# Squares product without Strassen, and a wait of GpSimd on VectorE's two-operand operations

## The chip, the cores and the metric

The kernel runs on one core of a Trainium2 chip. The metric is device time in microseconds (us), the median of several executions of the same program. Five engines run side by side and meet at semaphores: TensorE (PE; PEld is its weight load), VectorE (DVE), ScalarE (ACT), GpSimd (POOL) and SyncE (SP), which mainly issues transfers. ACT and POOL issue transfers too; the transfers that add to what already stands at their destination are issued by POOL.

## The reference

```python
out_lin = x @ lin_w.T + lin_b                                   # x: 1024 x 512
xv = jnp.einsum('bf,efm->bem', x, weight)                       # weight: 64 x 512 x 512
zp = jnp.einsum('bf,efm->bem', jnp.square(x), jnp.square(weight))
interaction = 0.5 * jnp.sum(jnp.square(xv) - zp, axis=1)
return out_lin + interaction                                    # 1024 x 512
```

All inputs are float32. Since the sum over e can be taken before the second product, the squares need only one product: square(x) times the sum over e of square(weight), a 1024 x 512 by 512 x 512 product. The first einsum is 64 times as large and is the bulk of the work.

## The kernel before

**Three stages on TensorE.** First the linear part, x times lin_w. Then the main stage, the products of x with all weights. Last the squares product. All results are kept transposed where that helps, and everything is split in halves in both matrix directions (quadrants A11, A12, A21, A22 of x; r counts the two halves of x's rows, which are the batch, and c the two halves of the output columns).

**Strassen.** All three products are done by one level of Strassen's scheme in Winograd's form: seven products of quadrants or of sums of quadrants in place of eight. `OPERAND` names the left operand of each of the seven: A11, A12, A22 and the sums R5, R6, R7, R3.

**Main stage.** The weights are taken in 32 parts (h = 0 to 31). For each part the seven products come in the order 1, 6, 2, 3, 7, 5, 4, where product 5 is already that of the next part. Each product has two halves of 512 batch rows (a pair of PSUM banks each, from a ring of four pairs `bank`). To get float32 accuracy from the fast fp32r matmul, each operand is written as pieces H (high), L (low) and K (a mixed small term), and a product is three passes: H times H and L times L are the "front", K times K is the "back". Between the front and the back the bank is scaled and added to (`stt`, line 367). The back of a product is issued `LAG` = 4 slots after its front. The pieces of the x operands (X1H to X7K) are made once at the start and stay. The pieces pH, pL, pK of the weights are made for each product by `split` (line 630): H by ACT, L by ACT and then POOL or DVE, K by POOL. They live in rings of three buffers. `finish` (line 683) squares the finished banks on ACT (`sq`) and reduces over e on DVE (`acc`). `w_squares` (line 623) squares the raw weights on ACT (`wsq`) and reduces them on DVE into `w2_sum`. For product 7, DVE first subtracts p5 from the bank (`w<-bank,p`).

**The squares product (lines 793 to 916).** `load_square` loads the quadrants of x again into free weight buffers, ACT squares them, and sums of them are built by ACT and adding transfers (`add_square`, `minus`). `column_sums` builds the sums of quadrants of `w2_sum` on POOL. Then `one_level` (line 505) issues the seven products 1, 2, 5, 6, 4, 7, 3 as plain float32 matmuls, line 523. The output tiles `o_name[r, c]` start as the linear part (`p<-lind`) plus the summed squares of xv (`p<-accd`, adding transfers on POOL), DVE adds the products into them (`into`, `columns`), and ACT's queue stores them.

**The order of the work.** `Plan` (line 41) holds all operations with costs and dependencies. TensorE's order is fixed by `key`. `forward` (line 146) lays out the other engines in modelled time, always the ready operation with the earliest due time (`latest`); `order` (line 123) repeats that 60 times with slightly moved due times and keeps the layout with the earliest modelled end. The program then issues each engine's operations in that order, so that on the chip each engine runs its list in order.

VectorE and GpSimd can block one another when VectorE reads two tensors from SBUF. Operations of that kind carry `both=True`. The plan lets such a VectorE operation stay `held` while GpSimd is busy, and it writes an extra wait (`op.after`, issued at line 921) into the next GpSimd operation in two cases:

```python
elif tensor and held is not None and held.latest < o.latest + self.YIELD:
    ends(DVE, held, now + held.costs[DVE])
    o.after, held = held, None
    ...
elif tensor and held is None and free[DVE] > now and running[DVE].both:
    o.after = running[DVE]
    ends(e, o, free[DVE] + cost)
```

In all other cases nothing but the data orders a GpSimd operation against VectorE's.

Of the kernel before, what the change touches and what calls it, by code (L numbers as in the profile page):

```python
# [18 lines left out]
P = 128  # L19
# [7 lines left out]
LAG = 4  # L27
ORDER = (1, 6, 2, 3, 7, 5, 4)
SPLIT = {**dict.fromkeys(range(1, 8), POOL), 2: DVE, 3: DVE}
X_SPLIT = {5: DVE, 6: DVE, 3: DVE, 7: DVE, 1: DVE, 2: "DMA", 4: "DMA"}  # L30
FIRST = {**dict.fromkeys(range(1, 8), POOL), 5: DVE}
SCALE = {1: "DVE", 5: "ACT"}
# [8 lines left out]
class Plan:  # L41
# [104 lines left out]
    def forward(self, chain):  # L146
# [4 lines left out]
        running = dict.fromkeys(pending)  # L151
        times = [self.HOP]
        done, late, nxt, wire, held, mark = [], 0.0, 0, [12.0], None, None

        def release(o):
            for e in o.costs:
# [52 lines left out]
        while len(done) < len(ops):  # L209
            now = heapq.heappop(times)  # L210
            moved = True
            while moved:
                moved = False
                for e in pending:
                    if free[e] > now + 1e-6:
                        continue
                    o = pick(e, now)
                    if e == POOL and held is not None and (o is None or o.move):
                        ends(DVE, held, now + held.costs[DVE])
                        held = None  # L220
                    if o is None:
                        continue
                    moved = True
                    if e == PE:
                        nxt += 1
                        if running[PE] and running[PE].emit:
                            mark = running[PE]
                        late = max(late, now - o.latest)
                    cost = o.costs[e]
                    o.start, o.engine = now, e  # L230
                    if o.move and o.emit and mark and now < self.EARLY[0] and now > max(
                        ready(o, e) + 0.3, free[e] + 0.1
                    ):
                        o.after = mark
                    tensor = e == POOL and not o.move
                    if e == DVE and o.both and free[POOL] > now + 0.05 and not running[POOL].move:
                        held, free[e], o.end = o, float("inf"), float("inf")
                    elif tensor and held is not None and held.latest < o.latest + self.YIELD:
                        ends(DVE, held, now + held.costs[DVE])
                        o.after, held = held, None  # L240
                        ends(e, o, free[DVE] + 0.15 + cost)
                    elif tensor and held is None and free[DVE] > now and running[DVE].both:
                        o.after = running[DVE]
                        ends(e, o, free[DVE] + cost)
                    else:
                        ends(e, o, now + cost)
                    for f in o.costs:
                        pending[f].discard(o.n)
                    done.append((o, e))
                    for x in o.succ:  # L250
                        left[x] -= 1
                        if not left[x]:
                            release(ops[x])
# [4 lines left out]
def kernel(  # L258
# [531 lines left out]


    out_dst = out.rearrange("(c p) b -> p c b", p=P)
    sq_home = {}
    for n, q in (("A21", "T"), ("A22", "w11"), ("A11", "w22"), ("A12", "w12")):
        sq_home[n] = raw[q]()
    for n, q in (("R5", "w11"), ("R6", "w21"), ("R3", "w12")):
        sq_home[n] = raw[q]()
    sq_home["R7"] = sq_home["A21"]

    def load_square(n, again=None):  # L800
        r, q = quads[n]
        o = sq_home[n]
        dma(buf[o], x_src[:, ts(q, KH), ts(r, H)], (), (o,))
        if again:
            act(buf[sq_home[again]], buf[o], AF.Square, (o,), (sq_home[again],))
        act(buf[o], buf[o], AF.Square, (o,), (o,))

    def add_square(n, m):
        o, i = sq_home[n], sq_home[m]
        dma_add(buf[o], buf[i], (i,), (o,))  # L810

    def minus(n, m):
        o, i = sq_home[n], sq_home[m]
        act(buf[o], buf[i], AF.Copy, (i,), (o,), scale=-1.0)

    load_square("A21")
    minus("A21", "A21")
    load_square("A22", "R5")
    add_square("R5", "A21")
    load_square("A11", "R6")  # L820
    add_square("R6", "R5")
    add_square("R7", "A11")
    load_square("A12")
    minus("R3", "A12")
    add_square("R3", "R6")
    w2 = {(r, c): w2_sum[:, ts(r, KH), ts(c, HM)] for r in range(2) for c in range(2)}
    w2_names = {z: (("w2h", *z),) for z in w2}
    for (r, c), ap in w2.items():
        plan.add({ACT: 0.6}, lambda _, ap=ap: nc.scalar.mul(ap, ap, -0.5),
                 tuple(("w2", r, m) for m in range(M)  # L830
                       if ("w2", r, m) in plan.writer and m // HM == c), w2_names[r, c])
    wt_home = [raw[q]() for q in ("w22", "T")]
    wt = {
        k: buf[wt_home[(k - 1) // 2]][:, (k - 1) % 2].rearrange("p (k m) -> p k m", k=KH)
        for k in range(1, 5)
    }
    wt_names = {k: (("wt", k),) for k in range(1, 5)}
    for z, n in enumerate(wt_home):
        used(n, ("wt", 2 * z + 1), ("wt", 2 * z + 2))
    column_sums(w2, wt, w2_names, wt_names,  # L840
                lambda o, a, b, r, w: pool(o, a, b, False, r, w, 512))
    act(wt[2], wt[2], AF.Copy, wt_names[2], wt_names[2], 512, -1.0)
    left = {i: (buf[sq_home[n]], (sq_home[n],)) for i, n in OPERAND.items()}
    right = rhs_of(w2, w2_names, wt, wt_names)

    turn(NG - 1)
    o_name = {}

    def acc_names(ch):
        return tuple(("accd", g, q) for g in range(NG) for q in range(P // MG)  # L850
                     if g * MG // P == ch)

    for (r, c), n in (((0, 0), "p1"), ((1, 0), "p1"), ((1, 1), "p5"), ((0, 1), "p5")):
        n = o_name[r, c] = kept[n]()
        for u in range(2):
            used((n, u), n)
        dma(buf[n], lin_dram[:, ts(c, 2), ts(r, H)], (("lind", r, c),), both_of(n))
        for u in range(2):
            ch = 2 * c + u
            if ch < M // P - 1:  # L860
                dma_add(buf[n, u], acc_dram[:, ch, ts(r, H)], acc_names(ch), ((n, u),), 1.4, 5.0)

    def into(n, bank, sub, u):
        o = buf[n][:, u]
        dve(o, o, buf[bank[u]], sub, ((n, u), bank[u]), ((n, u),))
# [5 lines left out]
    def columns(n, m, sub, u):  # L871
        o, i = buf[n][:, u], buf[m][:, u]
        dve(o, o, i, sub, ((n, u), (m, u)), ((n, u),), 512, True)

    v, f2, f5, f4 = four()
    f3 = f4[0], f2[0]
    key = slot[0]
    one_level(1, right, left, v, True, key)
    one_level(2, right, left, f2, True, key + 4)
    for u in range(2):  # L880
        into(o_name[0, 0], v, False, u)
        into(o_name[0, 0], f2, False, u)
        store(0, 0, u)
    one_level(5, right, left, f5, True, key + 6)
    z = kept["w"]()
    for u in range(2):
        used((z, u), z)
        act(buf[z, u], buf[f5[u]], AF.Copy, (f5[u],), ((z, u),), 512)
        for r in range(2):
            columns(o_name[r, 1], z, True, u)  # L890
    one_level(6, right, left, v, False, key + 8)
    for u in range(2):
        into(o_name[0, 1], v, True, u)
    one_level(4, right, left, f5, True, key + 11)
    for u in range(2):
        into(o_name[1, 0], f5, False, u)
    last = wsquare()
    for r in range(2):
        used((last, r), last)
    for r in (1, 0):  # L900
        dma(buf[last][:, r], acc_dram[:, M // P - 1, ts(r, H)], acc_names(M // P - 1),
            ((last, r),), 1.0)
        n = o_name[r, 1]
        stt(buf[n, 1], buf[last][:, r], 0.5, buf[n, 1], ALU.add, ((last, r), (n, 1)), ((n, 1),),
            512, True)

    one_level(7, right, left, v, False, key + 14)
    for u in range(2):
        into(o_name[1, 1], v, True, u)
        store(1, 1, u)  # L910
        into(o_name[1, 0], v, False, u)
        store(1, 0, u)
    one_level(3, right, left, f3, True, key + 17)
    for u in range(2):
        into(o_name[0, 1], f3, True, u)
        store(0, 1, u)

    for op, engine in plan.order():
        if op.emit:
# [40 lines left out]
```

## Time and profile before

| | |
|---|---|
| median of 3 runs | 1284.9 us (1284.19 to 1286.25) |
| the profiled execution, its own time | 1282.88 us |
| its span, first to last instruction | 1280.6 us |
| TensorE busy | 1275.7 us (100% of the span) |
| VectorE busy | 1230.9 us (96%) |
| ScalarE busy | 962.1 us (75%) |
| GpSimd busy | 1044.7 us (82%) |
| granted TensorE clock | 1.000 |

Matmuls are pipelined, so the busy time of one overlaps that of the next; what a matmul costs in a stream is the distance from one start to the next. A float32 matmul shows as two matmul records in the profile, an fp32r one as one record. Times after a line name (L702, L523) are from line numbers of the kernel before. "bank", "pL", "X6H" and the like are tile names with the buffer number left out; tiles that share storage show under the name of the storage, so that the squared quadrants appear as T and w, and the output tiles as p.

### The profile page before, as it was taken

The numbers are of one execution on the slowest core, as the hardware profiler recorded it, in microseconds if no ns is written. First come the engines' busy times: TensorE is split into PE (matmuls) and PEld (weight loads), VectorE is DVE, ScalarE is ACT, GpSimd is POOL, SyncE is SP. The second block draws the span as 40 slices with busy tenths as digits, with TensorE's granted clock in tenths as the row PEclk, the third lists the DMA queues.
The fourth block names the chain that finished last, engine by engine and source line by source line (L and its number), as shares of the span: only waits on it lengthen the run. The fifth ranks groups of instructions, "written<-read, shape, count | busy, mean of one in ns | idle before, by whom it ended". The sixth has DMA issues, their size and how long they took to land.

```text
span 1280.6 us, 15506 instructions
## 1 busy us (share of the span) xinstructions
PE 1275.7 (100%) x5484; PEld 1025.9 (80%) x5484; DVE 1230.9 (96%) x1021; ACT 962.1 (75%) x1006; POOL 1044.7 (82%) x531
## 2 busy tenths in 40 slices
PE   9999999999999999999999999999999999999998
PEld 4788888888888888888888888888888888888884
DVE  6999999999999999999999999999999999999996
ACT  7777787777887777877777877777788777778781
POOL 2988898888898888898888888888889888889891
PEclk9999999999999999999999999999999999999999
DMA  7765654455664555655445664545665445665656
GB/s 231 182 172 138 148 136 112 100 118 136 148 148 103 103 122 125 153 136 132 98 111 124 148 153 105 117 111 116 152 148 131 108 102 121 141 152 118 147 120 154
DMA packets 67645, 170.36 MB, mean 133 GB/s; under 512 B 22896, under 2 KB 23920, under 8 KB 67568
## 3 DMA queue, kind: packets, MB, share of 16 engines
q0 software_dynamic: 20160, 71.84, 30.5%
q1 hardware_dynamic: 45152, 94.39, 25.7%
q10 hardware_dynamic: 2256, 3.15, 0.7%
q8 instruction: 43, 0.70, 0.2%
q14 instruction: 34, 0.28, 0.1%
HBM read 158.86 MB, written 6.29 MB: 129 GB/s over the span
## 4 chain that ended last, share of the span: by engine, by line
PE 98%; DVE 1%; issue 0%; ACT 0%; ACTq 0%
PE bank L702 94%; PE bank L523 3%; PE bank L512 1%; DVE bank L367 0%; DVE acc L386 0%; PE bank L540 0%; DVE w_sum L386 0%; DVE w L373 0%; ACT sq L361 0%; DVE p L373 0%; ACTq L361 0%
## 5 line engine op out<-in xcount | busy, mean ns | idle before, releaser
L379 POOL TENSOR_TENSOR pK<-pH,pL 128x1024 fp32r<-128x1024 f32 x223 | 586.6, 2631 | 177.5 <-PE bank L702 169.4
L361 ACT ACTIVATE sq<-bank 128x1024 f32<-128x1024 f32 x256 | 261.6, 1022 | 95.4 <-issue 48.4
L386 DVE TENSOR_REDUCE acc<-sq 128x16 f32<-128x1024 f32 x256 | 308.0, 1203 | 0.7 <-ACT sq L361 0.7
L379 POOL TENSOR_TENSOR pL<-T,pL 128x1024 fp32r<-128x1024 f32 x95 | 237.9, 2504 | 1.0 <-ACT pL L361 1.0
L367 DVE SCALAR_TENSOR_TENSOR bank<-bank,w 128x1024 f32<-128x1024 f32 x192 | 234.1, 1219 | 0.4 <-PE bank L702 0.2
L373 DVE TENSOR_TENSOR w<-bank,p 128x1024 f32<-128x1024 f32 x128 | 155.6, 1216 | 26.0 <-PE bank L702 26.0
L379 POOL TENSOR_TENSOR pL<-w,pL 128x1024 fp32r<-128x1024 f32 x65 | 175.1, 2694 | 0.0
L361 ACT ACTIVATE p<-bank 128x1024 f32<-128x1024 f32 x128 | 131.0, 1023 | 56.3 <-PE bank L702 56.3
L367 DVE SCALAR_TENSOR_TENSOR pL<-pH,w 128x1024 fp32r<-128x1024 f32 x62 | 168.1, 2711 | 0.0
L361 ACT ACTIVATE pL<-T 128x1024 fp32r<-128x1024 f32 x95 | 100.0, 1053 | 74.5 <-issue 72.0
L386 DVE TENSOR_REDUCE w_sum<-wsq 128x16 f32<-128x1024 f32 x128 | 154.2, 1205 | 0.0
L367 DVE SCALAR_TENSOR_TENSOR bank<-bank,p 128x1024 f32<-128x1024 f32 x128 | 152.9, 1216 | 0.0
L361 ACT ACTIVATE pH<-w 128x1024 fp32r<-128x1024 f32 x127 | 134.2, 1057 | 11.6 <-PE bank L702 11.3
L361 ACT ACTIVATE wsq<-w 128x1024 f32<-128x1024 f32 x128 | 135.0, 1055 | 4.0 <-DVE w_sum L386 4.0
L361 ACT ACTIVATE pH<-T 128x1024 fp32r<-128x1024 f32 x96 | 101.3, 1055 | 0.0
L361 ACT ACTIVATE pL<-w 128x1024 fp32r<-128x1024 f32 x65 | 69.0, 1062 | 43.0 <-PE bank L702 25.0
L398 POOL DMA_DIRECT2D T<-weight x94 | 83.2, 978 | 9.2 <-POOL pL L379 9.0
L702 PE MATMUL bank<-pH,X4H 128*128 128x512 f32 x256 | 81.1, 397 | 0.1
L702 PE MATMUL bank<-pL,X4L 128*128 128x512 f32 x256 | 79.5, 391 | 0.0
L702 PE MATMUL bank<-pH,X5H 128*128 128x512 f32 x256 | 79.2, 391 | 0.0
L702 PE MATMUL bank<-pL,X5L 128*128 128x512 f32 x256 | 78.8, 389 | 0.0
L702 PE MATMUL bank<-pL,X6L 128*128 128x512 f32 x256 | 78.8, 389 | 0.0
(117 smaller groups left out, 2561.0 us busy)
## 6 DMA issues: line engine op xcount, KB each, us to landing
w<-weight SPq DMA_DIRECT2D x128, 512.0 KB, 7.7
T<-weight POOLq DMA_DIRECT2D x94, 512.0 KB, 7.4
w<-weight POOLq DMA_DIRECT2D x32, 512.0 KB, 10.3
T<-weight SPq DMA_DIRECT2D x31, 512.0 KB, 6.4
accd<-turned SPq DMA_DIRECT2D x64, 32.0 KB, 8.6
p<-lind SPq DMA_DIRECT2D x4, 512.0 KB, 6.2
out<-p ACTq DMA_DIRECT2D x8, 256.0 KB, 2.3
w<-xT SPq DMA_DIRECT2D x6, 256.0 KB, 4.9
```

What stands on the lines that cost most here:

```text
L361: nc.scalar.activation(o, i, func, bias=bias, scale=scale)
L367: return nc.vector.scalar_tensor_tensor(o, i, scalar, j, ALU.mult, op)
L373: return (nc.vector.tensor_sub if sub else nc.vector.tensor_add)(o, a, b)
L379: return (nc.gpsimd.tensor_sub if sub else nc.gpsimd.tensor_add)(o, a, b)
L386: lambda _: nc.vector.tensor_reduce(o, i.rearrange("p a (m e) -> p a m e", e=E), axis=AX.X, op=ALU.add),
L398: {POOL: 0.62}, lambda _: nc.gpsimd.dma_start(o, i, accum_op=ALU.add),
L512: return nc.tensor.matmul(buf[bank[u]], b[:, k, ts(u, P)], a[:, k, :], start=first and k == 0, stop=k == KH - 1, skip_group_check=True,)
L523: made = nc.tensor.matmul(buf[bank[u]], b[:, k, ts(u, P)], a[:, k, :], start=first and k == 0, stop=k == KH - 1, skip_group_check=True,)
L702: made = nc.tensor.matmul(buf[bank, j], buf[x][:, k, ts(2 * half + j, P)], buf[w][:, k, :], start=first and k == 0, stop=k == KH - 1, skip ...
```

## The change

Two things change.

The first is in `forward`. A variable `between` remembers the last two-operand VectorE operation that the plan has begun since the last GpSimd operation. When a GpSimd operation is laid out and has no extra wait yet, it gets one on that VectorE operation, even when the plan has it finished by then. The modelled times are not touched by this.

The second is the squares product. It is no longer Strassen's. The four output blocks (r, c) are computed one after the other, each as two products of quadrants (z = 0, 1), so eight block products, and each in three passes of fp32r matmuls on pieces H, L and K, as in the main stage. Passes 0 and 1 (H, L) of both z go to one pair of banks (`front`), pass 2 (K) to another (`back`); DVE scales each and adds it to the output tile. The pieces of the squares of x and of `w2_sum` are written over the x pieces X6, X2, X3 and X5, X1 of the main stage, which are not needed any more by then, and for A22 into one buffer of each ring of weight pieces. `SUMS` and `SQUARES` say who makes the L pieces: for `w2_sum` half 0 an adding transfer (the K piece too), for half 1 VectorE; for A11 and A12 GpSimd, for A21 and A22 an adding transfer. The K pieces of the squares are all made by GpSimd.

```diff
+SUMS = {0: "DMA", 1: DVE}
+SQUARES = {"A11": POOL, "A12": POOL, "A21": "DMA", "A22": "DMA"}
...
+        between = None
...
                     elif tensor and held is None and free[DVE] > now and running[DVE].both:
-                        o.after = running[DVE]
                         ends(e, o, free[DVE] + cost)
                     else:
                         ends(e, o, now + cost)
+                    if tensor:
+                        if o.after is None and between is not held:
+                            o.after = between
+                        between = held
+                    elif e == DVE and o.both:
+                        between = o
...
-    load_square("A21")
-    minus("A21", "A21")
...
-    column_sums(w2, wt, w2_names, wt_names,
-                lambda o, a, b, r, w: pool(o, a, b, False, r, w, 512))
...
+    for r, pieces in enumerate((("X5H", "X5L", "X5K"), ("X1H", "X1L", "X1K"))):
+        w2 = w2_sum[:, ts(r, KH)]
+        names = tuple(("w2", r, m) for m in range(M) if ("w2", r, m) in plan.writer)
+        sums[r] = h, l, k = pieces
+        act(buf[h], w2, AF.Copy, names, (h,), scale=-0.5 * TRIM)
+        if SUMS[r] == DVE:
+            stt(buf[l], w2, -0.5, f32(h), ALU.subtract, (h, *names), (l,), 1024, True)
+            stt(buf[k], f32(h), -U, f32(l), ALU.add, (h, l), (k,), 1024, True)
+        else:
+            half = (("w2h", r),)
+            act(w2, w2, AF.Copy, names, names + half, scale=-0.5)
+            act(buf[l], w2, AF.Copy, half, (l,), scale=-TRIM)
+            dma_add(f32(l), w2, half, (l,))
+            act(buf[k], w2, AF.Copy, half, (k,), scale=-U * TRIM)
+            dma_add(f32(k), f32(l), (l,), (k,))
+    for n, q, pieces in (
+        ("A11", "T", ("X6H", "X6L", "X6K")), ("A12", "w11", ("X2H", "X2L", "X2K")),
+        ("A21", "w22", ("X3H", "X3L", "X3K")), ("A22", "w12", [piece[z]() for z in "HLK"]),
+    ):
+        (r, z), o = quads[n], raw[q]()
+        dma(buf[o], x_src[:, ts(z, KH), ts(r, H)], (), (o,))
         act(buf[o], buf[o], AF.Square, (o,), (o,))
+        squares[r, z] = h, l, k = pieces
+        act(buf[h], buf[o], AF.Copy, (o,), (h,), scale=U * TRIM)
+        if SQUARES[n] == POOL:
+            act(buf[l], buf[o], AF.Copy, (o,), (l,), scale=TRIM)
+            pool(buf[l], buf[o], f32(l), True, (o, l), (l,))
+        else:
+            act(buf[l], buf[o], AF.Copy, (o,), (l,), scale=-TRIM)
+            dma_add(f32(l), buf[o], (o,), (l,))
+        pool(buf[k], f32(h), f32(l), True, (h, l), (k,))
...
-    for (r, c), n in (((0, 0), "p1"), ((1, 0), "p1"), ((1, 1), "p5"), ((0, 1), "p5")):
+    BLOCKS = (0, 0), (1, 0), (0, 1), (1, 1)
+    for (r, c), n in zip(BLOCKS, ("p1", "p1", "p5", "p5")):
...
+    def into(n, bank, scale):
+        stt(buf[n], buf[bank[0][0]], scale, buf[n], ALU.add, (*bank, *both_of(n)), both_of(n), 1024)
+
+    def into_half(n, bank, scale, u):
+        o = buf[n, u]
+        stt(o, buf[bank[u]], scale, o, ALU.add, (bank[u], (n, u)), ((n, u),))
...
-    one_level(1, right, left, v, True, key)
-    one_level(2, right, left, f2, True, key + 4)
...
+    def passes(which, r, c, bank, key):
+        for u in range(2):
+            for z in range(2):
+                def emit(_, u=u, z=z):
+                    for i in which:
+                        for k in range(KH):
+                            w, x = buf[sums[z][i]], buf[squares[r, z][i]]
+                            made = nc.tensor.matmul(
+                                buf[bank[u]], w[:, k, (2 * c + u) * P:(2 * c + u + 1) * P],
+                                x[:, k, :], start=z == 0 and i == which[0] and k == 0,
+                                stop=z == 1 and i == which[-1] and k == KH - 1,
+                                skip_group_check=True,
+                            )
+                    return made
+                reads = [t[i] for i in which for t in (sums[z], squares[r, z])]
+                plan.add({PE: len(which) * KH * PASS}, emit, (*reads, bank[u]), (bank[u],),
+                         key=key + 0.2 * u + 0.1 * z)
...
+    for at, (r, c) in enumerate(BLOCKS):
+        n = o_name[r, c]
+        front, back = b[2 * at % 4], b[(2 * at + 1) % 4]
+        passes((0, 1), r, c, front, key + 6 * at)
+        if at < 3:
+            into(n, front, S + 1.0)
+        if c == 1:
+            dma(buf[last][:, r], acc_dram[:, M // P - 1, ts(r, H)], acc_names(M // P - 1),
+                ((last, r),), 1.0)
+            stt(buf[n, 1], buf[last][:, r], 0.5, buf[n, 1], ALU.add, ((last, r), (n, 1)),
+                ((n, 1),), 512, True)
+        if at < 3:
+            passes((2,), r, c, back, key + 6 * at + 4)
+            into(n, back, S)
+        else:
+            into(n, front, S + 1.0)
+            back = back[0], b[0][1]
+            passes((2,), r, c, back, key + 6 * at + 4)
+            for u in range(2):
+                into_half(n, back, S, u)
+        for u in range(2):
+            store(r, c, u)
```

KH is 2 and P is 128: a pass of one u and one z is two matmuls of 128x128 weights and 512 columns.

More of the change, by code (lines that the diff above doesn't have):

```diff
@@ L792 @@
     out_dst = out.rearrange("(c p) b -> p c b", p=P)
[L793 to L805, printed above, removed]
-        act(buf[o], buf[o], AF.Square, (o,), (o,))
@@ L808, in add_square @@
[L808 to L814, printed above, removed]
-    load_square("A21")
-    minus("A21", "A21")
[L818 to L836, printed above, removed]
@@ L837 @@
-    wt_names = {k: (("wt", k),) for k in range(1, 5)}
-    for z, n in enumerate(wt_home):
-        used(n, ("wt", 2 * z + 1), ("wt", 2 * z + 2))
-    column_sums(w2, wt, w2_names, wt_names,
-                lambda o, a, b, r, w: pool(o, a, b, False, r, w, 512))
-    act(wt[2], wt[2], AF.Copy, wt_names[2], wt_names[2], 512, -1.0)
-    left = {i: (buf[sq_home[n]], (sq_home[n],)) for i, n in OPERAND.items()}
-    right = rhs_of(w2, w2_names, wt, wt_names)
+    squares, sums = {}, {}
+    for r, pieces in enumerate((("X5H", "X5L", "X5K"), ("X1H", "X1L", "X1K"))):
[13 more added lines that the diff above has]
+            dma_add(f32(k), f32(l), (l,), (k,))
@@ L846 @@
     turn(NG - 1)
-    o_name = {}
     def acc_names(ch):
@@ L851, in acc_names @@
                      if g * MG // P == ch)
-    for (r, c), n in (((0, 0), "p1"), ((1, 0), "p1"), ((1, 1), "p5"), ((0, 1), "p5")):
+    o_name = {}
+    BLOCKS = (0, 0), (1, 0), (0, 1), (1, 1)
+    for (r, c), n in zip(BLOCKS, ("p1", "p1", "p5", "p5")):
         n = o_name[r, c] = kept[n]()
@@ L861 @@
                 dma_add(buf[n, u], acc_dram[:, ch, ts(r, H)], acc_names(ch), ((n, u),), 1.4, 5.0)
-    def into(n, bank, sub, u):
-        o = buf[n][:, u]
-        dve(o, o, buf[bank[u]], sub, ((n, u), bank[u]), ((n, u),))
+    def into(n, bank, scale):
[3 more added lines that the diff above has]
+        stt(o, buf[bank[u]], scale, o, ALU.add, (bank[u], (n, u)), ((n, u),))
     def store(r, c, u):
@@ L869, in store @@
         dma(out_dst[:, 2 * c + u, ts(r, H)], buf[n, u], ((n, u),), (), 1.0, (SP, ACT))
[L871 to L877, printed above, removed]
-    one_level(1, right, left, v, True, key)
-    one_level(2, right, left, f2, True, key + 4)
[L880 to L896, printed above, removed]
+    def passes(which, r, c, bank, key):
[15 more added lines that the diff above has]
+                         key=key + 0.2 * u + 0.1 * z)
     last = wsquare()
@@ L899 @@
         used((last, r), last)
[L900 to L916, printed above, removed]
+    b = four()
+    key = slot[0]
+    for at, (r, c) in enumerate(BLOCKS):
[20 more added lines that the diff above has]
+            store(r, c, u)
     for op, engine in plan.order():
```

## The prediction

> **What bounds the kernel now.** I read the page's busy times first, then the chain of work that ended last, in order of time.
>
> ```profile
> PE 1275.7 (100%) x5484; PEld 1025.9 (80%) x5484; DVE 1230.9 (96%) x1021; ACT 962.1 (75%) x1006; POOL 1044.7 (82%) x531
> ```
>
> ```profile
> core 0 of [0], span 1280.6 us
> by line: PE bank L702 94.2%; PE bank L523 3.2%; PE bank L512 0.6%; DVE bank L367 0.4%; DVE acc L386 0.4%; PE bank L540 0.3%; DVE w_sum L386 0.2%; DVE w L373 0.2%; issue 0.1%; ACT sq L361 0.1%; DVE p L373 0.1%; ACTq L361 0.0%
> ...
> 66.84 1183.86 PE bank L702 x5208
> 1250.69 3.43 PE bank L523 x8
> 1254.13 1.86 PE bank L702 x8
> 1255.98 20.62 PE bank L523 x48
> 1276.60 0.02 issue
> 1276.62 0.69 DVE p L373
> ```
>
> TensorE at 100% proves little, since busy times of matmuls overlap. The chain proves it: from 66.84 us to 1276.60 it never leaves TensorE. VectorE is at 96% and GpSimd at 82%, yet neither ends a wait that the chain goes through. So only two things can move the time: fewer microseconds of matmuls, or new or removed waits of TensorE. How much waiting is left? The same chain asked for a late window alone gives the undisturbed step:
>
> ```profile
> 1224.86 25.84 PE bank L702 x114
> ```
>
> 25.84 / 114 = 0.2267 us from one fp32r matmul to the next. At that step the 5208 matmuls would take 1180.5 us; they took 1183.86. So 3.4 us, spread over the main stage, is all that better order could return there.
>
> **The matmuls.** The squares product now is line 523 after 1250 us: 3.43 + 20.62 = 24.05 us for 56 records, 28 float32 matmuls, 0.859 us each. The 1.86 us between are the last backs of the main stage and stay. New are 4 blocks x 2 u x 2 z x 3 passes x 2 = 96 fp32r matmuls, of the same form and size as those of line 702: 96 x 0.2267 = 21.76 us. The chain becomes shorter by 24.05 - 21.76 = 2.29 us. This is the main term. It is small because Strassen's saving (seven for eight) is given up while a float32 matmul costs 0.859 / 0.2267 = 3.8 passes and is replaced by three.
>
> The Trainium skill, "TensorE: Matmul & The Clock Gate", section "Wait — 56ns, not 53.3ns?", has warm back-to-back matmuls at N / 2.4 GHz plus about 2.5 ns, 0.2157 us for 512 columns; by that price the new product would be an estimated 20.7 us and the gain 3.3 us, over the bound for faster. The 5208 matmuls of this trace average 0.2273 us at the full granted clock, the new ones have the same form, and so I give that result no chance of its own.
>
> **The end.** After TensorE comes one VectorE addition, then a store.
>
> ```profile
> 1276.62 0.69 DVE L373 TENSOR_TENSOR p<-p,bank 128x512 f32<-128x512 f32 x1 [0.35 <-PE bank L523]
> ```
>
> ```profile
> L367 DVE SCALAR_TENSOR_TENSOR bank<-bank,p 128x1024 f32<-128x1024 f32 x128 | 152.9, 1216 | 0.0
> ```
>
> ```profile
> out<-p ACTq DMA_DIRECT2D x8, 256.0 KB, 2.3
> ```
>
> Let T be the end of TensorE. Now VectorE ends at T + 0.35 + 0.69 = T + 1.04. In the new last block the back is 8 matmuls, 1.81 us, so the front is done at T - 1.81 and its `into`, 1.22 us (price of the bank row), runs from T - 1.46 to T - 0.24. The two halves `into_half`, 0.69 each, follow: the first to T + 0.45, the second to T + 1.14. That is 0.10 us later. The stores keep number, size and landing time of 2.3 us; the last is one of eight as before. So +0.1.
>
> **What the new pieces cost the other engines.** Busy times of the last stretches:
>
> ```profile
> 1230.00:1240.00 10.00, 10.00 (x46) 8.28 (x45) 10.00 (x11) 8.99 (x11) 10.00 (x7) 1.00 0.63 132
> 1240.00:1250.50 10.50, 10.50 (x48) 8.60 (x47) 9.31 (x9) 4.60 (x5) 10.50 (x11) 1.00 0.83 164
> 1250.50:1276.60 26.10, 26.08 (x65) 11.98 (x64) 19.22 (x27) 4.05 (x5) 2.17 (x3) 1.00 0.59 145
> ```
>
> ```profile
> L361 ACT ACTIVATE w<-w 128x1024 f32<-128x1024 f32 x6 | 6.3, 1062 | 0.0
> ```
>
> The columns are PE, PEld, DVE, ACT, POOL. ScalarE: 12 operations for the four squares and 5 for `w2_sum`, 17 x 1.06 = 18.0 us, in place of eight squares and negations of the same price (8.5 us) and smaller ones: at most +9.5 us. It is idle for 1.0 + 5.9 us of the first two stretches and 22 us of the third, and only the pieces of A11, A12 and `w2_sum` are due by 1251. Cost on the path: nothing, under that cover; without it up to 9.5 - 6.9 = 2.6 us.
>
> ```profile
> L379 POOL TENSOR_TENSOR pK<-pH,pL 128x1024 fp32r<-128x1024 f32 x223 | 586.6, 2631 | 177.5 <-PE bank L702 169.4
> ```
>
> ```profile
> 1248.07 3.72 POOL L379 TENSOR_TENSOR T<-w_sum 128x512 f32<-128x512 f32 x1
> 1259.77 0.88 POOL L398 DMA_DIRECT2D p<-accd  x1 [7.97 <-DMA p<-lind]
> ```
>
> GpSimd: six subtractions of 2.63 us, 15.8 us, come in, and the four column sums (one is shown) go. The adding transfers are four before and four after, and the loads of x four and four. Due times, with the first new front at 1250.5: front 16 x 0.2267 = 3.63, old backs 1.81, so A11's K is due at 1255.9, A12's at 1256.4, A21's and A22's at 1261.4 and 1261.9; only the L of A11 and A12 are due by 1251. After 1250.5 the engine has 24 idle us now. Cost nothing, if the order in its queue is right (see the rivals).
>
> ```profile
> 1237.51 1.19 DVE L386 TENSOR_REDUCE w_sum<-wsq 128x16 f32<-128x1024 f32 x1
> ...
> 1246.35 1.22 DVE L386 TENSOR_REDUCE acc<-sq 128x16 f32<-128x1024 f32 x1 [0.36 <-ACT sq L361]
> 1248.01 1.22 DVE L373 TENSOR_TENSOR w<-bank,p 128x1024 f32<-128x1024 f32 x1 [0.44 <-PE bank L702]
> ```
>
> ```profile
> 1250.53 3.59 PE L523 MATMUL bank<-w,w_sum 128*128 128x512 f32 x8
> ```
>
> ```profile
> 1249.33 1.03 ACT L361 ACTIVATE sq<-bank 128x1024 f32<-128x1024 f32 x1 [1.68 <-DVE w L373]
> ```
>
> VectorE is the tight one. The last sum over `wsq` ends at 1238.70; then ScalarE makes H and VectorE makes L of half 1, due when z = 1 begins, 1250.5 + 0.9 = 1251.4. In that time VectorE also frees the first bank: `w<-bank,p` at 1248.01, ScalarE's square to 1250.36, and the tail's first matmul at 1250.53: under 0.2 us of play. L takes 1.2 us free and, behind a GpSimd operation, up to 3.4 us (next part). Its cover is the idle 0.36 and 0.44 and the reduction of 1.22, which nothing awaits at once: 2.0 us. So TensorE loses between 0 and 1.4 us here. I take 0.2, near the lower end, because the reduction alone covers an undisturbed L.
>
> **The new wait.** What is queued behind a waiting GpSimd operation is its whole list, and pK is what TensorE's backs need.
>
> ```profile
> L367 DVE SCALAR_TENSOR_TENSOR pL<-pH,w 128x1024 fp32r<-128x1024 f32 x62 | 168.1, 2711 | 0.0
> ```
>
> ```profile
> 416.89 3.02 POOL L379 TENSOR_TENSOR pK<-pH,pL 128x1024 fp32r<-128x1024 f32 x1
> 421.72 2.39 POOL L379 TENSOR_TENSOR pK<-pH,pL 128x1024 fp32r<-128x1024 f32 x1 [1.81 <-PE bank L702]
> ```
>
> ```profile
> 417.59 3.40 DVE L367 SCALAR_TENSOR_TENSOR pL<-pH,w 128x1024 fp32r<-128x1024 f32 x1
> ```
>
> ```profile
> 1225.29 1.78 DVE L367 SCALAR_TENSOR_TENSOR pL<-pH,w 128x1024 fp32r<-128x1024 f32 x1
> ```
>
> ```profile
> 1227.22 1.48 POOL L379 TENSOR_TENSOR w<-w_sum 128x512 f32<-128x512 f32 x1
> ```
>
> In the main stage the two-operand operations are these 62, two per part. At 417.59 VectorE begins while GpSimd works, and ends at 420.99, 1.08 us after GpSimd's 419.91: it was shut out. The next GpSimd subtraction starts at 421.72, 0.7 us after VectorE's end, because it awaited TensorE (a free buffer). The tightest of the 62 is the one at 1225.29: end 1227.07, GpSimd at 1227.22. In none does GpSimd begin inside one. The new wait is met before it is asked, 62 times. Cost zero; the collisions that exist are of the other kind (VectorE second), which this wait doesn't touch. If it did bind, GpSimd's 169 us of waiting for TensorE would cover it. Only at the start is there something to change:
>
> ```profile
> 36.20 3.22 POOL L379 TENSOR_TENSOR pK<-pH,pL 128x1024 fp32r<-128x1024 f32 x1 [1.25 <-DVE X6K L367]
> ```
>
> ```profile
> 35.95 1.21 DVE L373 TENSOR_TENSOR X7L<-w,X7H 128x1024 fp32r<-128x1024 f32 x1
> 37.09 3.42 DVE L373 TENSOR_TENSOR X3L<-w,X3H 128x1024 fp32r<-128x1024 f32 x1
> ```
>
> GpSimd began inside X7L, and X3L then lost 3.42 - 1.22 = 2.2 us to it. With the wait, VectorE could be up to 2.2 us earlier and GpSimd about 1 us later. Neither is on the chain there; I take zero, between a return of part of the 3.4 us (rival B) and +1.0.
>
> **Sum.** -2.29 + 0.10 + 0.2 + 0 = -2.0 us. Against the profiled execution: span 1280.6 to 1278.6, its time 1282.88 to 1280.9. The median of the runs is 2.0 above that execution, so 1284.9 becomes 1282.9, 0.16% less. About 0.2%, 2.57 us, is what a measurement of this kernel can tell from no change.
>
> **The rivals.** B, faster: the planner's list is laid out anew and the start is freed, and part of the 3.4 us lost in the main stage comes back too. At 0.6 of it the change passes 2.57; at 1.3 it gives 1281.6; all of it 1279.5. For it: VectorE's lost 2.2 us. Against: the loss recurs through the main stage, where the wait alters nothing. C, smaller gain: VectorE's L is shut out behind a GpSimd operation just before 1250, the full 1.4 us and, with K, as much again: 1284.1 to 1285.5. For it: that little play. D, slower: GpSimd's queue is in order, and its last `p<-accd` waited 7.97 us for a load, to 1259.77. If this one stands ahead of the K of A12, that K is ready only at 1259.8 + 0.9 + 2.6 = 1263.3, against 1256.4: TensorE waits 6.9 us, the sum is +4.7, 1289.6; with A11's K behind it as well 1292. If only A21's and A22's are behind, the loss is 4.0 us and the whole within the bound. It decides from 4.8 us of waiting. Against: the K pieces are due earlier than that addition, whose block now comes last, and the planner goes by due times; for: those are modelled times, and when a load lands is not in GpSimd's hands. E, the wait does nothing: that is in my sum already.
>
> **How the numbers follow.** Forecast 0.50 (1282.4 to 1283.5 by itself), B 0.23, C 0.14, D 0.13. Forecast and C lie within 0.2%: 0.64. The range 1281.2 to 1287.0 leaves out D (0.13) and the far end of B (0.06).
>
> **What would show it.** Right: the tail is 96 matmuls of 0.227 us without gaps, its first at about 1250.5; no waits of GpSimd for VectorE's pL in the table of waits; VectorE's last operation about 1.1 us behind the last matmul. Wrong: a gap of TensorE ahead of the first front or at a back, with GpSimd's pieces as releaser (D) or VectorE's L (C); a main stage under 1182 us (B); or a matmul step that differs in the tail.

## The result and the profile after

| | before | after |
|---|---|---|
| median (20 runs each) | 1284.45 us | 1281.99 us |
| lowest and highest run | 1282.77, 1286.25 us | 1281.12, 1283.26 us |
| the profiled execution, its own time | 1282.88 us | 1282.14 us |

The ratio is 0.9981, with a 95% interval of 0.9975 to 0.9987: 2.5 us less, between 1.7 and 3.2. That is about at the bound of what this kernel's measurement can tell from no change. Forecast were 1282.9 us, 2.0 us less.

The busy times of the kernel after, in the columns of the page:

```profile
PE 1274.3 (100%) x5524; PEld 1033.4 (81%) x5524; DVE 1233.0 (96%) x1014; ACT 967.0 (76%) x1008; POOL 1053.9 (82%) x533
```

No engine has changed its place. The count of TensorE is right for the change: 5484 - 56 + 96 = 5524. The chain of work that ended last, in order of time (start, duration, what), has changed at its end. Lines after the edit: 710 is the old 702, 870 issues the new passes, 375 is the old 367; in the experiments the numbers shift by a few lines.

```profile
67.63 1164.97 PE bank L710 x5126
...
1246.24 1.12 DVE acc L394
1247.36 2.62 DVE X1K L375
1249.98 1.15 DVE w L381
...
1251.21 1.03 ACT sq L369
...
1252.29 3.92 PE bank L870 x16
1256.21 1.81 PE bank L710 x8
1258.02 16.34 PE bank L870 x72
1274.38 1.24 DVE p L375
...
1275.71 0.69 DVE p L375
```

Before, the chain stood on TensorE up to the last addition. Now it leaves TensorE in front of the squares product, for VectorE: `X1K` (the K piece of the second half of `w2_sum`), then `w<-bank,p`, then ScalarE's square, which frees the bank that the first new front wants. The timeline of TensorE shows the hole that this makes (idle time before, and its releaser, in brackets):

```profile
1250.24 1.07 PE L710 MATMUL bank<-pK,X7K 128*128 128x512 f32 x4
1252.29 0.73 PE L870 MATMUL bank<-X6H,X5H 128*128 128x512 f32 x2 [0.97 <-ACT sq L369]
```

And the timelines of GpSimd and VectorE show why `X1K`, 1.2 us of work, took 2.71 us:

```profile
1245.53 3.36 POOL L387 TENSOR_TENSOR pK<-pH,pL 128x1024 fp32r<-128x1024 f32 x1
...
1250.07 2.97 POOL L387 TENSOR_TENSOR X6K<-X6H,X6L 128x1024 fp32r<-128x1024 f32 x1
```

```profile
1247.27 2.71 DVE L375 SCALAR_TENSOR_TENSOR X1K<-X1H,X1L 128x1024 fp32r<-128x1024 f32 x1
1249.90 1.21 DVE L381 TENSOR_TENSOR w<-bank,p 128x1024 f32<-128x1024 f32 x1
```

GpSimd's pK ends at 1248.89 and `X1K` ends 1.09 us behind it: it was shut out until pK had ended. X6K, which starts at 1250.07, is one of the operations that got the new wait.

Whole profiles can't be subtracted here: in these traces the main stage begins anywhere between 28.7 and 30.7 us, with the kernel before at 28.84 and 29.88 and the kernel after at 29.67 and 28.84. The stretches below are therefore taken from record to record inside each trace. "Gap" runs from the start of the last pK,X7K matmul to the start of the first squares matmul (0.23 is one step), "matmuls" from that pK,X7K to the start of the last matmul, "additions" from there to the end of VectorE, "end" from the issue of the last store to the end of the span. The last matmul record itself takes 0.43 us before (half a float32 matmul) and 0.23 after; it counts under additions. Three traces each of before and after, and all later kernels:

| kernel | gap | matmuls | additions | end |
|---|---|---|---|---|
| before (three: first, repeat, new wait alone) | 0.22, 0.23, 0.23 | 25.68, 25.69, 25.69 | 1.32, 1.32, 1.32 | 3.24, 3.24, 5.42 |
| after (three: first, two repeats) | 1.36, 1.42, 1.36 | 24.84, 24.90, 24.84 | 1.23, 1.23, 1.23 | 3.30, 3.32, 3.30 |
| squares alone | 12.51 | 37.32 | 1.23 | 3.67 |
| K late | 0.23 | 24.13 | 2.17 | 4.07 |
| both sums by transfers | 0.25 | 25.50 | 2.16 | 4.08 |
| K by transfer | 0.60 | 25.11 | 2.16 | 4.07 |
| stores late in the list | 1.36 | 24.85 | 1.71 | 3.32 |
| K 8 us earlier | 1.41 | 24.92 | 1.23 | 3.31 |
| K 15 us earlier | 0.23 | 23.64 | 2.16 | 4.08 |
| stores held | 1.38 | 24.88 | 1.72 | 4.77 |

From the last old back to VectorE's end, after has 26.1 us against 27.0: 0.9 less, made of 2.3 less for the matmuls by themselves, 1.15 more in the gap, 0.1 more in the first step behind it (0.34 us) and 0.1 more from the end of the last matmul to that of VectorE. The main stage, from the first X1H matmul to the last pK,X7K, is 1177.6 us against 1177.8, as means of three traces. Another 0.4 us lies outside the span: the time of a run exceeds its span by 2.1 to 2.4 us in every run of the kernel before whose span was kept, and by 1.7 to 2.0 in those of the kernel after and of all the changed kernels below, the new wait alone with the old squares product (1.79 to 1.95) among them. So this part doesn't come from the squares product, and its cause is open. What then remains of the 2.5 us lies behind the last store or isn't resolved; the experiments on stores look there.

### The profile page after: what moved, and what is told of

Its sections match the earlier page's. It is cut to its first block, busy times and chain, and to the rows that moved or that the text cites. A ratio compares the mean times of both kernels' runs of the same rounds, so it can differ in the third digit from the quotient of the medians.

```text
span 1280.3 us, 15588 instructions
## 1 busy us (share of the span) xinstructions
PE 1274.3 (100%) x5524; PEld 1033.4 (81%) x5524; DVE 1233.0 (96%) x1014; ACT 967.0 (76%) x1008; POOL 1053.9 (82%) x533
## 3 DMA queue, kind: packets, MB, share of 16 engines
q0 software_dynamic: 20160, 71.84, 30.7%
## 4 chain that ended last, share of the span: by engine, by line
PE 97%; DVE 2%; ACT 1%; issue 0%; DVEq 0%; ACTq 0%
PE bank L710 93%; PE bank L870 2%; PE bank L531 1%; DVE bank L375 1%; PE bank L520 1%; DVE acc L394 1%; PE bank L548 0%; DVE w L381 0%; ACT sq L369 0%; DVE w_sum L394 0%; DVE X1K L375 0%; DVE p L375 0%; DVE X1L L375 0%; ACT pL L369 0%; ACT pH L369 0%
## 5 line engine op out<-in xcount | busy, mean ns | idle before, releaser
L710 PE MATMUL bank<-pH,X6H 128*128 128x512 f32 x256 | 78.8, 389 | 0.0
```

Source lines behind the costliest of these rows:

```text
L710: made = nc.tensor.matmul(buf[bank, j], buf[x][:, k, ts(2 * half + j, P)], buf[w][:, k, :], start=first and k == 0, stop=k == KH - 1, skip ...
```

## The experiments

**The new wait alone**, in the kernel before.

```diff
+        between = None
...
-                        o.after = running[DVE]
...
+                    if tensor:
+                        if o.after is None and between is not held:
+                            o.after = between
+                        between = held
+                    elif e == DVE and o.both:
+                        between = o
```

> The kernel before with the new wait alone. Its instruction lists differ from the kernel before in a single place: the tenth subtraction or so of GpSimd in the start-up (pL from w22) now also waits for VectorE, whose operation there (X7K) ends about 1 us before GpSimd's subtraction starts anyway. Theory 1 (the wait is met before it is asked): no change, within 0.5 us of before, main stage 1184 us. Rival (the wait earns what the tail does not explain: the medians differ by 2.46 us, the two profiles' tails only by about 1.1 us): 1.0 to 1.4 us faster than before.

Measured: 1283.49 us against 1284.42, ratio 0.9995 (0.9987 to 1.0004). The chain's main row is the old one (1183.86 there):

```profile
68.33 1183.73 PE bank L708 x5208
```

By itself the wait does nothing that can be measured, in the main stage or at the start. That is a weak test of its cost: as the expectation says, only one GpSimd operation, at the start, gets a new wait in that kernel.

**The squares alone**, the change with `forward` as before.

```diff
-        between = None
...
+                        o.after = running[DVE]
...
-                    if tensor:
-                        if o.after is None and between is not held:
-                            o.after = between
-                        between = held
-                    elif e == DVE and o.both:
-                        between = o
```

> The changed kernel without the new wait (three GpSimd instructions lose one wait each, two of them in the tail: pK of the last product, and X6K, which waited for VectorE's X1K). Theory 1 (whoever waits for the port first gets it, so that X1K goes ahead of X6K without the wait too): as the changed kernel, 2.0 to 2.5 us below before, gap of TensorE ahead of the first new front about 1.0 us. Rival (GpSimd's next subtraction takes the port again when the former ends): X1K is shut out for another 2.5 to 3.0 us, the gap grows to 3 to 4 us, and the time is 0 to 0.7 us above before.

Measured, over four runs: 1295.47 us, ratio 1.0086 (1.0073 to 1.0099): 11 us slower than before and 13.5 slower than after. The timelines of VectorE and GpSimd:

```profile
1247.13 13.85 DVE L369 SCALAR_TENSOR_TENSOR X1K<-X1H,X1L 128x1024 fp32r<-128x1024 f32 x1
1260.91 1.21 DVE L375 TENSOR_TENSOR w<-bank,p 128x1024 f32<-128x1024 f32 x1
```

```profile
1245.40 3.41 POOL L381 TENSOR_TENSOR pK<-pH,pL 128x1024 fp32r<-128x1024 f32 x1
1247.76 1.88 POOL L400 DMA_DIRECT2D pL<-w  x1
1248.35 2.20 POOL L400 DMA_DIRECT2D p<-accd  x1
1248.91 4.01 POOL L381 TENSOR_TENSOR X6K<-X6H,X6L 128x1024 fp32r<-128x1024 f32 x1
1251.26 3.96 POOL L381 TENSOR_TENSOR X2K<-X2H,X2L 128x1024 fp32r<-128x1024 f32 x1
1253.54 3.42 POOL L400 DMA_DIRECT2D p<-accd  x2
1254.68 4.64 POOL L381 TENSOR_TENSOR X3K<-X3H,X3L 128x1024 fp32r<-128x1024 f32 x1
1256.96 3.19 POOL L400 DMA_DIRECT2D p<-accd  x1
1257.57 5.60 POOL L381 TENSOR_TENSOR pK<-pH,pL 128x1024 fp32r<-128x1024 f32 x1
```

The chain:

```profile
1247.21 13.77 DVE X1K L369
1260.98 1.15 DVE w L375
...
1262.21 1.03 ACT sq L363
...
1263.29 5.25 PE bank L864 x16
```

`X1K` is as far behind pK as in the kernel after, and pK ends at 1248.81. But X6K stands ready at 1248.91, and `X1K` lets it and the next ones pass: it ends only at 1260.98, after X3K (to 1259.32) and inside the record of the last pK. In the kernel after X6K waits for `X1K` by semaphore, and the loss is 1.1 us in place of 12.5. So the two parts of the change don't add up: 0 for the one, +11 for the other, -2.5 together. The wait is worth 13.5 us, nearly all of it at that one place: 11.1 us are the longer gap. Another 1.3 come right behind it, where the first 16 squares matmuls take 5.25 us in place of 3.92. TensorE's granted clock was 0.55 from 1263.29 to 1266.50 and 1.00 from 1268.54 on; in the kernel after, with its gap of 1.4 us, it was 1.00 throughout the tail.

**K late.** `X1K` is ordered behind the `w<-bank,p` that frees the first bank.

```diff
-            stt(buf[k], f32(h), -U, f32(l), ALU.add, (h, l), (k,), 1024, True)
+            stt(buf[k], f32(h), -U, f32(l), ALU.add, (h, l, value["w", NH - 1, 0]), (k,), 1024, True)
```

> The changed kernel, but VectorE's K piece of half 1 of the sums (X1K) may begin only after VectorE has freed the first bank (w<-bank,p of the last part's product 7). Theory 1 (the gap of 0.97 us of TensorE at the hand-over comes from X1K being shut out for 1.5 us ahead of that operation): the gap falls under 0.2 us and the time is 0.8 to 1.0 us below the changed kernel, about 3.4 us below before. Rival (the bank is freed late for another reason, or the gap moves to the first back because X1K is then late): no gain against the changed kernel, with TensorE waiting at the first back.

Measured: 1283.26 us, ratio 0.9993 (0.9985 to 1.0002). The gap is gone (0.23), but part of the loss comes back later. From the chain:

```profile
1251.28 1.24 DVE w L381
...
1252.54 1.23 DVE bank L375
1253.78 2.66 DVE X1K L375
1256.43 1.14 DVE acc L394
...
1257.66 1.03 ACT sq L369
...
1258.73 14.84 PE bank L870 x64
```

`X1K` is shut out at its new place too (2.66 us), and now it is the second block's bank that is late. The matmuls end 0.7 us sooner than in the kernel after (24.13 us against 24.84), but in this layout VectorE has more left behind them (2.17 us against 1.23), and the last store ends later (4.07 against 3.30); the two take more than that.

**Both sums by adding transfers**, so that VectorE makes no piece of `w2_sum`.

```diff
-SUMS = {0: "DMA", 1: DVE}
+SUMS = {0: "DMA", 1: "DMA"}
```

> The changed kernel with L and K of half 1 of the sums made by adding transfers, as for half 0, so that VectorE makes no piece in the tail at all. Theory 1 (VectorE's pieces make the gap): no wait for a bank at the hand-over; but L has to travel from 1240 us on and is due at 1251.4, and transfers of this size take 7 to 10 us here, so L is met narrowly and K (due at 1257) by 1 to 3 us not: between 0.8 us below and 2 us above the changed kernel. Rival (the gap is not VectorE's): gap of about 1 us at the first front as in the changed kernel.

Measured: 1284.94 us, ratio 1.0006 (0.9997 to 1.0016). The gap is 0.25, but the chain now runs through GpSimd's queue:

```profile
1259.25 9.13 DMA p<-accd
...
1268.56 1.24 DVE p L375
1269.84 3.94 PE bank L870 x16
```

The two more transfers push the `p<-accd` back; one lands 9.1 us after its issue, VectorE's addition waits for it and TensorE for the bank.

**Only K by a transfer.**

```diff
-            stt(buf[k], f32(h), -U, f32(l), ALU.add, (h, l), (k,), 1024, True)
+            act(buf[k], f32(h), AF.Copy, (h,), (k,), scale=-U)
+            dma_add(f32(k), f32(l), (l,), (k,))
```

> The changed kernel, but K of half 1 of the sums (X1K) is made by ScalarE and an adding transfer in place of VectorE; L stays with VectorE. Theory 1 (X1K shut out on VectorE makes the gap at the hand-over; with K off VectorE nothing takes its place, since K is due only at 1257): gap under 0.2 us, 0.8 to 1.0 us below the changed kernel, about 1281.0. Rival (another adding transfer among those on GpSimd's queue delays the additions to the output tiles, as when both pieces went by transfer, where TensorE waited 1.6 us ahead of the third block): no gain.

Measured: 1284.51 us, ratio 1.0004 (0.9995 to 1.0013). The gap falls to 0.60, and GpSimd's last piece is late:

```profile
1255.13 3.73 POOL p L406 x2
...
1261.55 3.02 POOL pK L387
1264.61 10.78 PE bank L871 x46
```

This is rival D's mechanism in small: transfers issued by GpSimd ahead of its K pieces.

**The kernels before and after, one more execution each**, to see which differences of single traces return.

> The kernel before, unchanged, for a second profile. The two profiles on hand differ by 0.74 us, the medians by 2.46. Theory 1 (the first profile of before was a short one at its end: six stores are queued there one behind another and their landing varies): from the last store's issue to the end of the span over 4 us here, against 3.26 in the first profile; PE's part as in the first, within 0.2 us, once the start-up loads are taken out. Rival (the difference is in the start-up loads alone): 3.2 to 3.4 us at the end, and the first product of the main stage (28.84 in the first profile) a us or more later.

> The changed kernel, unchanged, for a second profile. Theory 1: the end after the last store's issue 3.2 to 3.5 us as in its first profile, since its stores are spread over the last 14 us; gap of TensorE ahead of the first new front 0.9 to 1.2 us again. Rival (the end varies by itself, whatever the stores): over 4 us at the end.

Measured: 1283.93 us and 1281.43 us. The stretches of the table return within about 0.1 us, all but the start of the main stage, which moved from 28.84 to 29.88 in the one and from 29.67 to 28.84 in the other.

**The stores of the second and third block late in the list.**

```diff
-    def store(r, c, u):
+    def store(r, c, u, *also):
...
-        dma(out_dst[:, 2 * c + u, ts(r, H)], buf[n, u], ((n, u),), (), 1.0, (SP, ACT))
+        dma(out_dst[:, 2 * c + u, ts(r, H)], buf[n, u], ((n, u), *also), (), 1.0, (SP, ACT))
...
+            for r2, c2 in BLOCKS[1:3]:
+                for u in range(2):
+                    store(r2, c2, u, (n, 0))
```

> The changed kernel with the four stores of the second and third output block held back until the last block's front has been added, so that six stores stand together at the end as in the kernel before (even closer). Theory 1 (stores that queue at the end cost about 1 us of the kernel before's time): 1.5 to 2.5 us above the changed kernel. Rival (the last store lands in 2 us whatever is queued ahead of it): no change, within 0.5 us.

Measured: 1282.73 us, ratio 0.9993 (0.9984 to 1.0002). A miss: the added dependency shifted the place in the list, but the stores went out as soon as their data stood, as in the kernel after. It says nothing on the stores. (Its additions end 0.5 us later.)

**X1K due 8 us earlier**, and 15 us, so that it stands ahead of the operations of GpSimd that shut it out.

```diff
+            plan.ops[-1].early = 8.0
...
-            o.latest = latest
+            o.latest = latest = latest - getattr(o, "early", 0.0)
```

> The changed kernel with the due time of X1K set 8 us earlier in the plan. VectorE's order near the hand-over stays the same; what changes is that GpSimd's pK of the last product now waits for X1K, so that VectorE is first at the port. Theory 1 (the gap at the hand-over is X1K shut out by that pK): X1K takes 1.2 us in place of 2.7, the gap of TensorE falls from 1.1 to under 0.2 us, and the time is 0.9 to 1.1 us below the changed kernel. Rival (the gap is set by something else as well, or pK, now later, becomes late for TensorE's last backs): gap or a new wait of about 1 us, no gain.

> The same with 15 us: X1L and X1K both move ahead of two reductions and of GpSimd's X6L and X2L, which then wait for VectorE. Theory 1: gap under 0.2 us, 0.9 to 1.1 us below the changed kernel, if the main stage's last products are not held up by VectorE's earlier pieces. Rival: VectorE, busy to 96%, is late with the banks of the products before, and TensorE waits 1 us or more there.

Measured: 1281.88 us, ratio 0.9986 (0.9977 to 0.9995), and 1285.91, ratio 1.0015 (1.0006 to 1.0024); the kernel after, timed beside them, has 1282.20. VectorE with 8 us:

```profile
1243.58 2.07 DVE L375 SCALAR_TENSOR_TENSOR X1L<-w_sum,X1H 128x1024 fp32r<-128x1024 f32 x1
...
1247.83 1.99 DVE L375 SCALAR_TENSOR_TENSOR X1K<-X1H,X1L 128x1024 fp32r<-128x1024 f32 x1
```

and with 15 us:

```profile
1237.75 2.55 DVE L375 SCALAR_TENSOR_TENSOR X1L<-w_sum,X1H 128x1024 fp32r<-128x1024 f32 x1
...
1241.36 2.57 DVE L375 SCALAR_TENSOR_TENSOR X1K<-X1H,X1L 128x1024 fp32r<-128x1024 f32 x1
```

In the first, X1L is now shut out as well, and together they lose about as much as X1K did alone. In the second both lose 1.35 us, but ahead of the last banks of the main stage, which ends 2.1 us later; the gap is gone and the matmuls behind it run without any loss (23.64 us, 104 steps), but later additions and stores take that again (2.16 and 4.08 us in the table). The loss moved with the two operations; neither place was free of it.

**The stores of the second and third block truly held** until the last block's first addition (the same edit as with the late stores, and a wait written by hand):

```diff
+                    plan.ops[-1].hold = plan.writer[n, 0]
...
+        if hasattr(op, "hold"):
+            tc.add_manual_dep(
...
```

> The changed kernel with the four stores of the second and third block now truly held (by a wait) until VectorE has added the last block's front; in the earlier try the order of the list alone did not hold them. Theory 1 (stores that queue behind one another at the end are the part of the kernel before's time that the tail of TensorE does not explain): from the last store's issue to the end of the span 1.5 to 3 us more than the changed kernel's 3.3, and the time up by 1 to 3 us. Rival (the last store lands in 2 us whatever is queued): no change within 0.5 us.

> The changed kernel, unchanged, timed beside the three others on the same chip. It should come out 1.7 to 2.5 us below before; its gap of TensorE at the hand-over again 1.0 to 1.2 us (a rival would be that the gap differs from execution to execution).

Measured: 1284.36 us, ratio 1.0004 (0.9995 to 1.0013), and for the unchanged kernel after 1282.20, ratio 0.9987 (0.9978 to 0.9996). This repeat gives the change 1.4 us, with an interval of 0.5 to 2.8, where the first measurement gave 2.5. Holding the stores costs 2.2 us; in the traces 0.5 of it lies in the additions and 1.5 behind the last store. The 0.5 stands in the kernel with the stores late in the list too, whose stores were not held, so only the 1.5 is the price of the bunching. Issues of stores in ScalarE's queue, first of the kernel before, then of the one after:

```profile
1260.18 0.96 ACTq L393 DMA_DIRECT2D out<-p  x2
...
1273.91 3.77 ACTq L393 DMA_DIRECT2D out<-p  x6
```

```profile
1263.51 13.86 ACTq L401 DMA_DIRECT2D out<-p  x5
```

Before, six of the eight stores go out within 3.8 us at the end. After, they are spread over 13.9 us (three more in SyncE's queue, from 1263.50), because the four blocks are finished one behind the other.

## Why the prediction was right

**The matmuls: right.** 2.29 us were forecast. The row of 72 gives 16.34 / 72 = 0.2269 us a step, against the 0.2267 taken from the main stage. From the first of the 96 to the last, with the eight old ones between, the starts lie 23.48 us apart. That is 0.11 over 103 such steps, all of it in the first step, which took 0.34. The 0.2157 us of the Trainium skill ("TensorE: Matmul & The Clock Gate", section "Wait — 56ns, not 53.3ns?") are not seen here either; with them this row would be an estimated 15.5 us.

**The hand-over: mis-sized.** I took 0.2 from a range of 0 to 1.4, "because the reduction alone covers an undisturbed L". It cost 1.15 us. L was undisturbed (X1L took 1.22), and it was K that was shut out, ahead of the `w<-bank,p` on which the bank hangs. No matmul needs this K before 1258.31, and I priced it only in rival C. So C's mechanism came true, with K in L's place and 1.15 of its 1.4 us. The mark that I named for C, a gap ahead of the first front with VectorE's L as releaser, is there but for the piece: the profile names ScalarE's `sq`, and the chain leads on to `X1K`.

**The new wait: right in the main stage, wrong in the tail.** "Met before it is asked, 62 times" held as far as it was tried: the wait alone moves nothing, though it adds a wait to a single operation there, and in the table of waits of the kernel after no operation of GpSimd waits for VectorE's pL. But I asked only whether it could cost. "The collisions that exist are of the other kind (VectorE second), which this wait doesn't touch" is the step that failed. It rested on the row at 417.59, in which VectorE got in as soon as the running subtraction had ended. There GpSimd had nothing ready behind it. With a queue of ready subtractions behind it, in the kernel without the wait, VectorE's operation was held not for one of them but for several, and the wait bounds just that. My bound for a shut-out operation was 3.4 us; without the wait it took 13.85. The total came out because in the kernel as changed the wait stands exactly there, which I had not seen: that part was luck.

**The end: right for VectorE, open for the stores.** +0.10 was forecast for VectorE's end behind the last matmul. It was 1.32 - 0.43 = 0.89 us and is 1.23 - 0.23 = 1.00: +0.11. But "the stores keep number, size and landing time" overlooked when they go out. With the last six bunched, 3.24, 3.24 and 5.42 us passed from the last issue to the end in three traces of the old layout; spread, 3.30 to 3.32. So in two traces of three the bunched stores ended no later than the spread ones; in the third the last store landed 3.9 us after its issue, against 2.0. That fits the runs' spread, 3.5 us from lowest to highest before and 2.1 after, but doesn't show that the bunching is the cause. The held stores show that bunching can cost 1.5 us, though they bunch more tightly than the kernel before does.

**The sum.** Tail -0.9, main stage -0.15, outside the span -0.4: together about 1.45 us, which the repeats bear out. That is under the interval of the first measurement (1.7 to 3.2) and just what the repeat gave (1.4). The end would add 0.7 on average of three traces, all of it from the one long end, which makes 2.1; the remaining 0.3 us of the first median have not been placed. The -2.0 was near the result with errors of opposite sign in it: a hand-over 0.95 too cheap, against 0.4 outside the span that no term foresaw and stores that were to change nothing and may have given back about 0.7. That these nearly cancel is luck. The forecast 1282.9 also starts from 1284.9, the median of the first three runs, where 20 runs gave 1284.45.

**The rivals.** B fell: the main stage did not speed up (1177.6 us against 1177.8; with the wait alone its chain row is 1183.73 against 1183.86). D fell in the kernel as changed: X2K, the K of A12, was ready at 1255.39 and needed at 1258.31, because the planner put no `p<-accd` ahead of it that waits long. It showed how near it was when a transfer or two were added: TensorE then waited for GpSimd's queue in both experiments.

## What to carry to other kernels

Price an operation that two engines fight over by what its rival has ready behind the running instruction, not by the running instruction alone; if a queue stands ready there, a wait of the rival on your operation can be worth far more than the operation itself takes (13.5 us here, for one of 1.2). A gain on the engine that bounds the kernel must be followed through the first hand-over that it reaches, with every operation queued ahead of the one that frees the buffer. When a product is split into blocks that finish one by one, count the stores that are still to go at the end, too: four of them held back cost 1.5 us here.

## What the runs showed of the hardware

A VectorE operation with two operands in SBUF that comes second to GpSimd need not be next in line when the running GpSimd operation ends. With more subtractions ready on GpSimd, `X1K` took 13.85 us in the squares-alone kernel, and at least three of them that began after it went first. This is the only such place in the fourteen traces. In the kernel with both sums by transfers a pL at 78.33 did get in (to 80.61), with GpSimd's running subtraction ending at 79.53 and its next one beginning at 80.09. There 0.56 us lay between the two; where `X1K` was passed by, 0.10 lay between pK's end and X6K's start. The Trainium skill ("SBUF — State Buffer", section "Who interferes with whom") has an exclusive lock: whoever issues first holds it for the whole instruction and the other is blocked. The trace agrees for one against one (1.09 us from pK's end to `X1K`'s in the kernel after). It disagrees with the reading that the block ends with that instruction, by which `X1K` would have been done near 1250.0 in the squares-alone kernel and not at 1260.98. What let it in at last, ahead of the end of the fifth subtraction, the traces don't tell, and GpSimd's records overlap there.
